# Five kinds of transfers change their issuing engine: from SyncE to GpSimd, in a fused kernel of four layers

## The chip, the core and the metric

The kernel runs on one core of a Trainium2 chip. A core has five engines with an instruction stream of their own: TensorE (PE in the profile, with its weight loads as PEld), VectorE (DVE), ScalarE (ACT), GpSimd (POOL) and SyncE (SP). Sixteen DMA engines move data between the device's memory and the core's on-chip memory. An engine's instructions start in the order of its stream, and a transfer is started by an instruction in the stream of the engine that issues it. The metric is the device time of one execution in microseconds; the profile also gives the clock that TensorE was granted.

## The reference

The input x has shape (16, 32, 128, 128): 16 images of 32 channels. Four layers follow, each of the form x = x + layer(gn(x)), where gn normalises the channels of an image in 16 groups:

```python
x = x + _L0_conv_ref(_gn(x), ...)   # row LSTM over skewed columns: 128 steps of gates
x = x + _L1_conv_ref(_gn(x), ...)   # adder network: -sum |patch - w| over 3x3x32, quantised to 8 bit
x = x + _L2_conv_ref(_gn(x), ...)   # Hartley transform, 32x32 modes mixed across channels, and back
x = x + _L3_conv_ref(_gn(x), ...)   # five edge operators, normalised; small U-shaped net; times its input
```

Layer 3 ends with `return orig * y`, where y comes from conv1 on 160 edge channels, three poolings, conv2 to conv4, and three 2x2 upsamplings each followed by a 3x3 convolution. All outputs are float32.

## The kernel before

The program has three stages in time. `stage0` computes layer 0 for all images. Then `Differences` computes layer 1, image by image, while `After` computes layers 2 and 3 for groups of four images (g = 0 to 3) in the background. What is left when layer 1 ends is done by `drain`.

**Layer 1.** For each half of an image there are 72 tiles (8 groups of output channels by 9 taps) of 128 partitions by 64 rows. A tile is made either by VectorE (L705, a float16 subtract and max into `d_dve`) or by ScalarE (L702, a ReLU into `d_act`), and TensorE sums it over the channels with 16 matmuls (L592). Loads of the quantised image `q` (L559), of raw rows `xq` (L536) and of the residual `xr1` (L566), the store of quantised rows (L552) and the store of the layer's output x2 (L579) are issued by SyncE.

**The background.** `Weave` is a planner at build time. It keeps an estimate in microseconds of where PE, DVE and ACT stand, and places pieces of `After`'s work between the tiles of layer 1. A piece can be put off: `weave.later(us, step)` says that `step` becomes due so many estimated microseconds from now. Transfers are put off this way too, so their place in the stream of the issuing engine follows the plan, and on the chip the issuing engine waits at that place until the transfer may start. Once this is written out, `keep_order` fixes every engine's order as it stands. In the drain, two such planners (one with the rest of groups 0 to 2, one with group 3) take turns, and after that the framework keeps the order of the program.

**A group's way through layers 2 and 3.** `forward` loads x2, transforms it and mixes the modes (loads of mode weights L1114, stores and loads of small matrices L1041, L1092, L1151). It clears its tile `xs` by two GpSimd memsets (L983, L984). `back` transforms the mixed modes back, adds them to x2, 16 pieces of 512 KB a group, and stores x3: `residual` loads a piece (L1169), `take_out` adds and takes statistics on VectorE (L1213, L1215), and `store` writes it back (L1219) and later reloads the buffer for the piece four further on. `encoder` then reads x3 twice. `frames` keeps a ring of two chunks of 20 rows, each 128 partitions by 20 by 132 float32; a half chunk is loaded by `load` (L1277, up to 10 rows of 512 bytes for each partition) and normalised in place by ScalarE (L1283), with edges set by ScalarE copies and, at the first and last row of an image, a GpSimd memset (L1286). The first pass, `statistics`, feeds matmuls at L1323 and copies the image's sides (L1353); the second, `conv1`, feeds matmuls at L1638. After the last half chunks of the first pass the loads of the second pass's first chunks follow. Between them, SyncE loads `gm` (L1311, L1389), which VectorE uses at L1383, and folded weights `v` (L1435), used at L1450. `small_layers` loads its weights at L766 and L835. `last` works on four units of 32 rows: `load` reads x3 in four transfers of 32 partitions each (L1708), TensorE makes the last upsampling (L849, L874), VectorE multiplies (L1766, L1729), ScalarE adds the mean (L1739), and `store` writes the output in four transfers (L1745).

All of these transfers are issued by SyncE, in one stream; only three small constant loads at the start come from ScalarE's queue. GpSimd does memsets and one reduction over partitions.

Of the kernel before, what the change touches and what calls it, by code (L numbers as in the profile page):

```python
# [15 lines left out]
B, C, H, W = 16, 32, 128, 128  # L16
# [27 lines left out]
def bc_view(t, g):  # L44

    return t.rearrange("b c h w -> (b c) (h w)")[g * 128 : (g + 1) * 128]
# [856 lines left out]
class After:  # L903
# [250 lines left out]
    def back(self, g, load):  # L1154


        nc, tc, cst, d, weave = self.nc, self.tc, self.cst, self.d, self.weave
        x2, x3, z_d = d["x2"], d["x3"], d["z"]

        with self.pool("t_z") as zp_, self.pool("t_r", 4) as rp:  # L1160

            def rows(n):

                first = g * 4 * CHW + (4 * (n // 2) + 64 * (n % 2)) * W
                return lambda t: bass.AP(t.tensor, t.offset + first, [[HW, 128], [32 * W, 2], [1, 4 * W]])

            def residual(n):
                xr.append(rp.tile([128, 2, 4 * W], F32, name="xr2"))
                nc.sync.dma_start(xr[n], rows(n)(x2))  # L1169

            xr = []
            stat = zp_.tile([128, 32, 6], F32, name="stat3")
            zi = zp_.tile([128, 32, 32], F32, name="zi")
            for blk in range(4):
                first = z_d.offset + (4 * g + blk) * 32768
                nc.sync.dma_start(
                    zi[32 * blk : 32 * blk + 32], bass.AP(z_d.tensor, first, [[32, 32], [1024, 32], [1, 32]])
                )
            for n in range(4):
                residual(n)  # L1180
            yield -12.0

            o1 = zp_.tile([128, 32, 4, 32], F32, name="o1")
            for oh in range(2):
                pa = [self.acc() for _ in range(4)]
                for o in range(16):
                    for r in range(4):
                        for blk in range(4):
                            part = slice(32 * blk, 32 * blk + 32)
                            nc.tensor.matmul(  # L1190
                                pa[blk][32 * r : 32 * r + 32, 32 * o : 32 * o + 32],
                                zi[part, 16 * oh + o, :],
                                cst["cas_t"][part, 32 * r : 32 * r + 32],
                                start=True,
                                stop=True,
                            )
                    yield 1.1
                yield SUMMED
                for blk in range(4):
                    dst = o1[:, :, blk, 16 * oh : 16 * oh + 16].rearrange("p h o -> p o h")  # L1200
                    src = pa[blk].rearrange("p (o h) -> p o h", h=32)
                    nc.vector.tensor_copy(dst, src)
                weave.dve += 2.6
                yield -2.0

            ready = {}

            def take_out(n, pf):
                while ready.get(n):
                    weave.done(ready[n])  # L1210
                for r in range(2):
                    v = xr[n][:, r]
                    nc.vector.scalar_tensor_tensor(v, pf[r], 2.0**-15, v, ALU.mult, ALU.add)  # L1213
                for r in range(2):
                    nc.vector.bn_stats(stat[:, 2 * n + r, :], xr[n][:, r])  # L1215
                weave.dve += 2.8

                def store():
                    nc.sync.dma_start(rows(n)(x3), xr[n])  # L1219
                    ready[n + 4] = weave.later(6.0, lambda: reload(n + 4)) if n < 12 else None  # L1220

                ready[n + 4] = weave.later(4.0, store)

            def reload(n):
                residual(n)
                ready[n] = None

            previous = None
            for n in range(16):
                s, half = n // 2, n % 2  # L1230
                pf = [self.acc() for _ in range(2)]
                for i in range(4):
                    for r in range(2):
                        part = slice(64 * half + 32 * r, 64 * half + 32 * r + 32)
                        nc.tensor.matmul(  # L1235
                            pf[r][:, W * i : W * i + W],
                            o1[part, 4 * s + i].rearrange("p b o -> p (b o)"),
                            cst["cas_t"][part, :],
                            start=True,
                            stop=True,  # L1240
                        )
                yield 0.8
                if previous:
                    yield -4.5
                    take_out(*previous)
                previous = n, pf
            yield SUMMED
            take_out(*previous)
            weave.later(7.0, lambda: [load(ch, half) for ch in range(2) for half in range(2)])
            mv = zp_.tile([128, 1, 2], F32, name="mv3")  # L1250
            nc.vector.bn_aggr(mv[:, 0, :], stat.rearrange("p a b -> p (a b)"))
            yield from normalised(nc, zp_, self.ps, weave, mv, 1, cst["avg2_bc"], 1e-5, self.stats3)
            nc.vector.scalar_tensor_tensor(
                self.shift3, self.stats3[:, 0], -1.0, self.stats3[:, 1], ALU.mult, ALU.mult
            )
            yield -2.5

    def frames(self, g, pool):

        nc, x3, weave = self.nc, self.d["x3"], self.weave
        ring = [pool.tile([128, 20, W + 4], F32, name=f"xp{i}") for i in range(2)]
        for t in ring:
            nc.vector.memset(t[:, :, 0], 0.0)
            nc.vector.memset(t[:, :, W + 3], 0.0)

        def parts(ch, half):

            lo, hi = max(16 * ch - 2 + 10 * half, 0), min(16 * ch + 8 + 10 * half, H)
            off = lo - (16 * ch - 2)
            return ring[ch % 2], lo, hi, ring[ch % 2][:, off : off + hi - lo, 2 : W + 2]

        def load(ch, half):
            t, lo, hi, v = parts(ch, half)
            nc.sync.dma_start(v, bc_view(x3, g).rearrange("p (h w) -> p h w", w=W)[:, lo:hi, :])  # L1277

        def normalise(ch, half, us):
            t, lo, hi, v = parts(ch, half)  # L1280

            def step():
                nc.scalar.activation(v, v, AF.Identity, bias=self.shift3, scale=self.stats3[:, 1])  # L1283
                for edge, r, src, zero in ((lo == 0, 1, 3, 0), (hi == H, 18, 16, 19)):
                    if edge:
                        nc.gpsimd.memset(t[:, zero, :], 0.0)  # L1286
                        nc.scalar.copy(t[:, r, 2 : W + 2], t[:, src, 2 : W + 2])
                own = slice(10 * half, 10 * half + 10)
                nc.scalar.copy(t[:, own, 1], t[:, own, 3])  # L1289
                nc.scalar.copy(t[:, own, W + 2], t[:, own, W])  # L1290
                weave.act += 2.0

            return weave.later(us, step)

        chunk = lambda ch: ring[ch % 2]
        return load, normalise, chunk

    def statistics(self, g, pool, frames, sides, out, tables):
# [395 lines left out]
    def last(self, g):  # L1694

        nc, tc, cst, weave = self.nc, self.tc, self.cst, self.weave
        with self.pool("l_y") as yp, self.pool("l_x", 2) as xp:
# [3 lines left out]
            def at(t, unit, j):  # L1701
                first = t.offset + g * 4 * CHW + (32 * unit + 8 * j) * W
                return bass.AP(t.tensor, first, [[HW, 32], [CHW, 4], [1, 8 * W]])

            def load(unit):
                xr = xp.tile([128, 4, 8 * W], F32, name="xr3")
                for j in range(4):
                    nc.sync.dma_start(xr[32 * j : 32 * j + 32], at(self.d["x3"], unit, j))  # L1708
                return xr

            xr = [load(0), load(1)]

            rhs = yp.tile([128, 2, 4], F32, name="l_rhs")
            nc.vector.tensor_tensor(rhs, bcast(self.stats3[:, :, 0], 2, 4), bcast(cst["m4_bc"], 1, 2), ALU.mult)
            yield -2.0
            p = self.acc()
# [25 lines left out]

            def store(x, unit):
                for j in range(4):
                    nc.sync.dma_start(at(self.out, unit, j), x[32 * j : 32 * j + 32])  # L1745
                following[unit] = weave.later(10.0, lambda: reload(unit)) if unit < 2 else None

            def reload(unit):
                xr[unit] = load(unit + 2)
                following[unit] = None  # L1750
# [5 lines left out]
            for unit in range(4):  # L1756
                complete(unit - 2)
                x = xr[unit % 2]
# [186 lines left out]
```

## Time and profile before

| What | Value |
|---|---|
| Time, median of 3 runs | 7221.99 us (7218.79 to 7231.17) |
| Span of the profiled execution | 7207.9 us, 272193 instructions |
| Mean granted TensorE clock | 0.891 |
| Busy: PE, PEld | 5763.4 us (80%), 3183.3 us (44%) |
| Busy: DVE, ACT, POOL | 5804.1 us (81%), 5477.6 us (76%), 34.7 us |
| Bytes moved by DMA | 722.55 MB, mean 100 GB/s |
| Transfers at the five lines of the change | 64 each at L1169, L1219, L1708, L1745; 128 at L1277 |

Busy time is what an engine spends on instructions; an instruction that waits, branches or issues a transfer from SyncE or ScalarE is not counted. In groups of instructions, `xr<-acc` names the tile written and the tile read, `x64` is the number of instructions, and after the bar stand the busy time in us, the mean ns of one, the idle time of the engine just before them, and what ended most of it. In the list of waits, a row gives who waited, for whom, the total in us, how many times and the longest. `SPq` means SyncE's queue: all of SyncE's time is waiting or issuing.

### The profile page before, as it was taken

To read this page: it belongs to the slowest core of one execution; us is meant where nothing else is said; L and a number is where in the kernel's file an instruction comes from. 1 tells how busy PE (TensorE), PEld (TensorE's weight loads), DVE (VectorE), ACT (ScalarE), POOL (GpSimd) and SP (SyncE) were. 2 spreads that over 40 slices of the span, in tenths; PEclk is the share of its full clock that TensorE was granted. 3 is DMA by queue.
4 is the path that set the end of the run, shared out by engine and by line. 5 is a ranking of instruction groups with operands and counts; after the bars stand their busy time and mean duration, and the time that the engine had idled before them with its cause. 6 is when DMAs were issued, how large, how long until landed. Compare 5 with 4: busy or idle time off the path is not lost. (4 is left out here: it accounts for less than half of the span.)

```text
span 7207.9 us, 272193 instructions
## 1 busy us (share of the span) xinstructions
PE 5763.4 (80%) x128140; PEld 3183.3 (44%) x128140; DVE 5804.1 (81%) x7016; ACT 5477.6 (76%) x3147; POOL 34.7 (0%) x31
## 2 busy tenths in 40 slices
PE   4878567777888786999778786899888787698985
PEld 3665333333344342333334443333334466546653
DVE  7787689999999998999899998999989882513234
ACT  2555489999999998999999998999999851032322
POOL 0000000000000000000000000000000000000000
PEclk9899889999988898999888988999988876699997
DMA  8664211111133343111253344211134245531234
GB/s 310 227 207 142 84 63 57 56 58 46 48 94 102 127 110 93 64 55 49 53 133 94 99 139 109 72 55 59 35 101 116 85 130 163 163 105 57 65 70 114
DMA packets 374322, 722.55 MB, mean 100 GB/s; under 512 B 50896, under 2 KB 219856, under 8 KB 362320
## 3 DMA queue, kind: packets, MB, share of 16 engines
q1 hardware_dynamic: 372768, 704.58, 31.8%
q8 instruction: 1002, 16.42, 1.0%
q14 instruction: 120, 0.98, 0.0%
q10 hardware_dynamic: 432, 0.57, 0.0%
HBM read 507.21 MB, written 164.32 MB: 93 GB/s over the span
## 5 line engine op out<-in xcount | busy, mean ns | idle before, releaser
L702 ACT ACTIVATE d_act<-q,neg 128x8192 f16<-128x8192 f16 (+1 forms) x622 | 4398.3, 7143 | 204.1 <-PE acc L592 154.9
L705 DVE TENSOR_SCALAR d_dve<-q,qw 128x8192 f16<-128x8192 f16 (+1 forms) x1682 | 3877.4, 2362 | 166.4 <-PE acc L592 124.1
L592 PE MATMUL acc<-d_dve,sel 128*32 128x512 f16 x26912 | 1882.1, 403 | 512.9 <-DVE d_dve L705 458.9
L592 PEld LDWEIGHTS <-sel 128*32 128x32 f16 x36864 | 1027.2, 100 | 2137.7 <-issue 1482.8
L1638 PE MATMUL acc<-xp,wf 32*32 32x512 f32 x25600 | 1034.2, 616 | 36.5 <-issue 26.7
L592 PE MATMUL acc<-d_act,sel 128*32 128x512 f16 x9952 | 732.2, 417 | 315.1 <-ACT d_act L702 306.5
L1638 PEld LDWEIGHTS acc<-xp,wf 32*32 32x32 f32 x25600 | 418.5, 104 | 397.0 <-issue 319.5
L1577 ACT ACTIVATE y<-pooled,b 32x128 f32<-32x128 f32 x512 | 204.7, 400 | 396.3 <-DVE pooled L1563 247.3
L622 PE MATMUL acc<-q,zero 128*32 128x512 f16 x7008 | 503.0, 398 | 0.0
L207 PE MATMUL pg<-h,wb 64*64 64x20 f32 (+15 forms) x4096 | 398.4, 322 | 104.7 <-DVE h L256 63.3
L1283 ACT ACTIVATE xp<-xp,shift,stats 128x1280 f32<-128x1280 f32 (+1 forms) x128 | 182.4, 1434 | 358.2 <-DMA xp<-x_d 356.1
L849 PE MATMUL acc<-y,u_conv 32*32 32x256 f32 (+1 forms) x9728 | 359.4, 466 | 69.7 <-issue 45.1
L244 ACT ACTIVATE gt<-pg,bias 128x20 f32<-128x20 f32 (+15 forms) x1024 | 316.9, 375 | 81.4 <-PE pg L207 74.2
L207 PE MATMUL pg<-e,wb 64*64 64x20 f32 (+15 forms) x4096 | 354.7, 316 | 16.7 <-DVE e L260 5.6
L207 PEld LDWEIGHTS pg<-h,wb 64*64 64x64 f32 x4096 | 250.6, 155 | 139.3 <-DVE h L256 88.7
L622 PEld LDWEIGHTS <-zero 128*32 128x32 f16 x7008 | 211.9, 101 | 195.6 <-issue 40.5
L207 PE MATMUL pg<-xn,wb 64*64 64x28 f32 (+61 forms) x4096 | 286.6, 304 | 11.3 <-ACT gt L244 3.5
L207 PEld LDWEIGHTS pg<-e,wb 64*64 64x64 f32 x4096 | 253.0, 157 | 92.5 <-DVE e L260 62.9
L1323 PE MATMUL acc<-xp 32*64 32x204 f32 (+3 forms) x8576 | 249.9, 359 | 31.3 <-ACT xp L1289 22.9
L255 ACT ACTIVATE th<-c 128x20 f32<-128x20 f32 (+15 forms) x256 | 81.3, 320 | 235.1 <-DVE c L253 233.7
L849 PEld LDWEIGHTS acc<-y,u_conv 32*32 32x32 f32 x9728 | 171.1, 111 | 193.1 <-issue 139.3
L1739 ACT ACTIVATE xr<-xr,l_ms 128x1024 f32<-128x1024 f32 x64 | 70.0, 1141 | 221.9 <-DVE xr L1729 199.3
(208 smaller groups left out, 4607.3 us busy)
## 6 DMA issues: line engine op xcount, KB each, us to landing
xr<-x_d SPq DMA_DIRECT2D x192, 512.0 KB
xp<-x_d SPq DMA_DIRECT2D x112, 640.0 KB
q<-q_d SPq DMA_DIRECT2D x32, 2145.0 KB
x_d<-xr SPq DMA_DIRECT2D x128, 512.0 KB
x_in<-in_x_dram SPq DMA_DIRECT2D x16, 2048.0 KB
res<-in_x_dram SPq DMA_DIRECT2D x64, 512.0 KB
xn<-in_xs_dram SPq DMA_DIRECT2D x64, 512.0 KB
xn<-xn SPq DMA_DIRECT2D x128, 256.0 KB
```

The costliest lines, as they stand in the source:

```text
L207: nc.tensor.matmul(bank[c][q][64 * pair : 64 * pair + 64, :, :width], wb[half, 4 * kind + KIND[q]].rearrange("p b o -> p (b o)"), v[half], ...
L244: nc.scalar.activation(gt[:, q, :, :n], bank[c][q][:, :, :n], AF.Tanh if q == G else AF.Sigmoid, bias=bias[:, KIND[q] : KIND[q] + 1],)
L255: nc.scalar.activation(th[:, :, :n], cell, AF.Tanh)
L592: self.nc.tensor.matmul(acc[k][32 * j : 32 * j + 32, :], self.sel16[:, i // 9, :], d[:, row : row + 4, c : c + W], start=first, stop=last,)
L622: self.nc.tensor.matmul(acc[k][32 * j : 32 * j + 32, :], self.zero, q[:, :4, :W], start=False, stop=False)
L702: nc.scalar.activation(dst, src, AF.Relu, bias=self.neg[:, i : i + 1])
L705: nc.vector.tensor_scalar(dst, src, self.qw[:, i : i + 1], 0.0, ALU.subtract, ALU.max)
L849: nc.tensor.matmul(acc[blk][32 * j : 32 * j + 32, o : o + rows * n], t[part, 4 * par + tap, :], src[part, top : top + rows, left : left + ...
L1283: nc.scalar.activation(v, v, AF.Identity, bias=self.shift3, scale=self.stats3[:, 1])
L1323: nc.tensor.matmul(gram[blk][j : j + width, at : at + n], xp[part, l, 2 + j : 2 + j + width], xp[part, rows, j : j + width + 4], start=sta ...
L1577: nc.scalar.activation(d, s, AF.Identity, bias=bj)
L1638: nc.tensor.matmul(acc[blk][32 * j : 32 * j + 32, :], tap_of("all", tap)[rows], xp[rows, 4 * j + kh : 4 * j + kh + 4, kw : kw + W], start= ...
```

## The change

Five transfer lines are issued by GpSimd instead of SyncE: loads and stores of `back`, loads of `frames`, and loads and stores of `last`. All other transfers stay with SyncE. It is meant to split one stream into two, so that a transfer that has to wait for its engines does not stand before transfers of another part of the program. Sizes, addresses, buffers and the plan are the same.

```diff
             def residual(n):
                 xr.append(rp.tile([128, 2, 4 * W], F32, name="xr2"))
-                nc.sync.dma_start(xr[n], rows(n)(x2))
+                nc.gpsimd.dma_start(xr[n], rows(n)(x2))
...
                 def store():
-                    nc.sync.dma_start(rows(n)(x3), xr[n])
+                    nc.gpsimd.dma_start(rows(n)(x3), xr[n])
...
         def load(ch, half):
             t, lo, hi, v = parts(ch, half)
-            nc.sync.dma_start(v, bc_view(x3, g).rearrange("p (h w) -> p h w", w=W)[:, lo:hi, :])
+            nc.gpsimd.dma_start(v, bc_view(x3, g).rearrange("p (h w) -> p h w", w=W)[:, lo:hi, :])
...
                 for j in range(4):
-                    nc.sync.dma_start(xr[32 * j : 32 * j + 32], at(self.d["x3"], unit, j))
+                    nc.gpsimd.dma_start(xr[32 * j : 32 * j + 32], at(self.d["x3"], unit, j))
...
                 for j in range(4):
-                    nc.sync.dma_start(at(self.out, unit, j), x[32 * j : 32 * j + 32])
+                    nc.gpsimd.dma_start(at(self.out, unit, j), x[32 * j : 32 * j + 32])
```

## The prediction, before the change was run

> **What bounds the kernel now.** I read the slices first, then busy time by stage, then the costliest groups, then who waits for whom, and last single stretches of the trace.
>
> The kernel's page, busy tenths in 40 slices of 180 us, one row an engine:
>
> ```profile
> PE   4878567777888786999778786899888787698985
> ...
> DVE  7787689999999998999899998999989882513234
> ACT  2555489999999998999999998999999851032322
> ```
>
> Three stages: the recurrence (to about 1050 us), the differences of layer 1 with the back work of layers 2 and 3 woven in (to 5860), and a drain (the last 1348 us). The second stage is two thirds of the time, and there VectorE (DVE) and ScalarE (ACT) are both full; in the drain they are a quarter to a half busy and TensorE (PE) leads. Busy us of each engine in the last two stages:
>
> ```profile
> 1050.00:5860.00 4810.00, 3972.41 (x82426) 1902.86 (x82422) 4540.25 (x3610) 4616.92 (x1213) 27.22 (x15) 0.91 0.27 80
> 5860.00:7208.00 1348.00, 1077.25 (x31330) 755.64 (x31322) 460.54 (x1110) 298.12 (x561) 5.10 (x9) 0.81 0.41 113
> ```
>
> After the length come PE, its weight loads, DVE, ACT and POOL (GpSimd): DVE is idle for 4810 - 4540 = 270 us of the second stage, ACT for 193. What fills DVE there, by shape, with the mean ns of one:
>
> ```profile
> L705 DVE TENSOR_SCALAR d_dve<-q,qw 128x8192 f16<-128x8192 f16 x1053 | 2447.4, 2352 | 90.6 <-PE acc L592 89.6
> L705 DVE TENSOR_SCALAR d_dve<-q,qw 128x8320 f16<-128x8320 f16 x576 | 1371.1, 2380 | 35.6 <-PE acc L592 34.5
> ```
>
> 8192 elements a partition in 2352 ns are 3.5 per ns. A float32 subtract of 2048 elements (L1014) takes 2284 ns, 0.9 per ns: L705 runs in a fast mode, some four times as fast an element.
>
> The change is about the queue. SyncE's longest waits in the second stage (us in total, times, longest):
>
> ```profile
> SPq L552 <- DVE qt L549: 939.7, 47, 43.5
> SPq L579 <- DVE xr L573: 697.7, 51, 86.4
> SPq L1277 <- PE acc L1638: 307.8, 11, 65.4
> SPq L1745 <- ACT xr L1739: 199.5, 8, 84.2
> SPq L1219 <- DVE xr L1213: 160.1, 26, 53.2
> ```
>
> It stands for hundreds of us with everything later behind it, and the last three rows move. But what it delays has slack: in this stage ACT waits only 2.8 us in 4 waits for frames (L1283), and DVE's waits for any transfer add up to about 70 us: gm (L1383) 33.0, xw (L1099) 26.1, folded weights (L1450) 8.1, xh 4.0. The queue could return little there.
>
> The last view decides. Two clears by GpSimd, beside DVE:
>
> ```profile
> 3742.00 1.90 POOL L983 MEMSET xs<- 64x2048 f32 x1 [520.21 <-PE acc L849]
> 3743.94 1.99 POOL L984 MEMSET xs<- 64x2048 f32 x1
> ...
> 3742.20 1.99 DVE L549 TENSOR_SCALAR qt<-qt 128x1040 f16<-128x1040 f16 x1
> 3744.11 6.26 DVE L705 TENSOR_SCALAR d_dve<-q,qw 128x8192 f16<-128x8192 f16 x2
> ```
>
> The f16 clamp L549, 0.43 us elsewhere, takes 1.99 and ends with the first clear; the two L705 take 6.26 instead of 4.70. The only three L705 over 2.5 us in the run are about 3.97 us, and all lie at such clears (1566.8, 1570.7 and 3744.1 us). It works both ways: the row clear L1286 takes 0.21 us in the drain and 2.17 to 3.22 in four places beside L705. So DVE's fast mode and GpSimd exclude each other, and here one waits for the other.
>
> [...]
>
> **The change part by part.** 320 transfers move, 80 for each of four groups of images: L1169 16, L1219 16, L1277 32, L1708 16 and L1745 16. By the trace 196 of them are issued before 5860 us (36, 32, 64, 32, 32), 124 in the drain. Bytes and arithmetic stay.
>
> 1. *Lost by DVE in the second stage.* [...] DVE waits h whenever its next instruction is a fast one. The fast ones are busy (3754 + 39 + 26)/4810 = 79% of the stage. h is not shown. Low end: 0.2 us, the shortest row clear, so 196 x 0.2 x 0.79 = 31 us. High end: the frame loads are 1280 pieces of 512 B (128 partitions x 10 rows) where the others have 128 or 256; [...] DVE's 270 idle us hide some 6% of that, leaving 145. Rows behind it cannot overtake: each engine's order in this stage is fixed, PE waits for L705 (287 waits between 1150 and 5890 us) and ACT's next tiles for PE.
>
> 2. *Gained in the second stage.* At 4422 us a 2145 KB q load stands behind frame loads, and then blocks the next issue by 30 us:
>
> ```profile
> 4422.48 0.37 SPq L1277 DMA_DIRECT2D xp<-x_d  x1
> 4423.19 0.55 SPq L559 DMA_DIRECT2D q<-q_d  x1
> 4427.72 0.36 SPq L1277 DMA_DIRECT2D xp<-x_d  x1
> 4428.14 31.14 SPq L1435 DMA_DIRECT2D v<-fold_d  x3
> 4459.38 1.38 SPq L1389 DMA_DIRECT2D gm<-in_gram_dram  x2
> ```
>
> DVE then sits idle for gm for 21.9 us. Without L1277 ahead of it the q load leaves earlier and the jam is likely over. I count 20 us. A like jam at 5582, which costs DVE 22.1 us at L1099, has no moved transfer in it and stays.
>
> 3. *Gained in the drain.* The chain shows two places:
>
> ```profile
> 5995.05 18.12 DMA xm_d<-xm
> 6013.18 0.50 SPq L1092
> ...
> 6015.38 14.83 DMA xp<-x_d
> ```
>
> Frame loads wait behind L1092, which waits for another group's store; PE is idle 22.0 us here, 15 of which go. At 7025.64 to 7030.79 four output stores (L1745) hold up a weight load (L766) for which PE then idles 10.7 us; 10 go. Together 25.
>
> 4. *Lost in the drain.* A frame load takes 4.2 us from issue to ACT's start where nothing else holds it, but the ring is two chunks deep, about three half chunks of 9 us ahead, so 1 to 5 us more stay hidden behind PE's other products. The store-and-reload of back (L1219, L1169) is exposed where PE waits for L1213: [...] the memsets L1286 behind transfers on GpSimd, [...] I take 10 in all.
>
> Frames in the second stage have 14 to 36 us from issue to use in nearly all cases; [...] SyncE's 0.36 us an issue saves nothing: it is idle anyway.
>
> Sum: 145 - 20 - 25 + 10 = +110; with 7222 that is 7332, say 7335.
>
> **The rivals.**
> - *The queue is relieved and DVE loses nothing* [...]: -20 - 25 + 10 = -35, 7187. For it: [...] the waits on SyncE are long. Against: the clears, and that little waits for those transfers.
> - *It cancels*: h at the low end, 31 - 35, 7218.
> - *GpSimd starves instead*: DVE's fast instructions run back to back, [...] With ten turns of 2.35 us a frame lands 24 us late; over a lead of 14 to 20 us that is some 8 us on ACT for each of the 32 loads of statistics in the stage, 250 us, about 7470. For it: L1286 at 3.22 us, 15 times its free time. Against: it still ran after one instruction, not ten.
>
> **How the numbers follow.** DVE loses about a microsecond for each transfer: 0.57, 7335. Relief alone: 0.26, 7187. Cancels: 0.09. Starved: 0.08. Faster by over 0.2% (below 7208) is the second, 0.26; within 0.2%, 0.10; slower 0.64. The range runs from a little below full relief, 7165, as the jams may be worth more than I found, to the high end of h: 357 x 0.94 = 336, less 35, is 7523, [...] part of the starved case, 7550.
>
> **What would show it.** Right: in the second stage the mean L705 rises from 2.36 us, with many at 3 to 4 us; the stage grows by about 110 to 140 us and the drain shrinks by some 15; the gaps at gm and before L766 are gone. POOL shows 320 more instructions of about 1 us. Wrong: L705 keeps its 2.35 us with stage and drain both a little shorter (relief), or keeps it while ACT's idle before L1283 grows in the second stage (starved). It would also be wrong if frames become late in the drain, where I have counted 10 us.

## The result, and the profile after

The changed kernel takes 7276.0 us (median, 7268.1 to 7291.1), beside 7220.4 us for the kernel before in the same comparison: a ratio of 1.0079, 95% interval 1.0057 to 1.0102. It is about 56 us slower, half of the 113 us forecast.

The stretches of the changed kernel's trace, cut where layer 1 ends (5906 us here, 5862 before); after the length come the busy us of PE, its weight loads, VectorE (DVE), ScalarE (ACT) and GpSimd (POOL), then the granted clock, the share of the DMA engines and GB/s:

```profile
1050.00:5906.00 4856.00, 3962.57 (x82557) 1892.41 (x82546) 4558.21 (x3608) 4618.86 (x1213) 354.52 (x211) 0.92 0.27 80
5906.00:7289.00 1383.00, 1071.76 (x31202) 749.18 (x31188) 458.42 (x1109) 294.57 (x561) 143.44 (x197) 0.81 0.39 110
```

The second stage grew by 44 us between these two executions, the drain by 38. That is more than the 56 us of the medians, since the profiled execution of the kernel before (7210.6 us) is a fast one of its kernel and that of the changed one (7291.1 us) the slowest of four. DVE's busy time in the stage rose only from 4542 to 4558 us. GpSimd's issues now count as busy: 355 us in the stage. The groups of L705 and of the moved loads and stores in that stage (busy us, mean ns of one, idle before):

```profile
L705 DVE TENSOR_SCALAR d_dve<-q,qw 128x8192 f16<-128x8192 f16 x1053 | 2458.1, 2362 | 100.3 <-PE acc L592 99.3
...
L705 DVE TENSOR_SCALAR d_dve<-q,qw 128x8320 f16<-128x8320 f16 x576 | 1374.6, 2386 | 51.5 <-PE acc L592 50.0
L1277 POOL DMA_DIRECT2D xp<-x_d x64 | 120.1, 1878 | 1310.4 <-PE acc L1638 917.2 <-PE acc L1323 156.0 <-DVE d_dve L705 69.1
```

L705 went from 2352 to 2362 ns and from 2380 to 2386. A frame load takes GpSimd 1878 ns on average in the stage; in the drain, where no L705 runs, the same instruction takes 0.95 us. One such meeting in the timeline of the changed kernel (start, us, engine and line; "x3" joins three instructions that follow each other):

```profile
2608.32 7.32 DVE L705 TENSOR_SCALAR d_dve<-q,qw 128x8320 f16<-128x8320 f16 x3
2608.94 2.31 POOL L1277 DMA_DIRECT2D xp<-x_d  x1 [7.31 <-PE acc L592]
```

The load starts inside the first L705 and ends 0.6 us after the second began (at 2610.61). The second takes 2.73 us, the others 2.37. So GpSimd waits for the running L705 to end, and then holds the next for 0.4 us. Of the 1682 L705 in this trace, 32 are over 2.5 us beside a frame load, at 2.65 to 2.81 us; over 2.35 us that is 12.3 us in all. No transfer of the other four lines stretches one that far. Seven shorter VectorE instructions beside frame loads of the stage (copies at L1353, clamps at L549) are longer too, by some 3 us together. The clears at L983 and L984 still do, as before; one pair of them now falls beside L705 where it did not, for 3.6 us more.

The jam at the q load is the same, though it looks different. VectorE waits for gm in the changed kernel's timeline:

```profile
4446.59 0.76 SPq L559 DMA_DIRECT2D q<-q_d  x1
4447.40 7.84 SPq L1435 DMA_DIRECT2D v<-fold_d  x3
4471.98 5.35 SPq L1389 DMA_DIRECT2D gm<-in_gram_dram  x2
...
4507.72 0.60 DVE L1383 TENSOR_TENSOR es_w<-acc,gm 128x420 f32<-128x420 f32 x1 [22.98 <-DMA gm<-in_gram_dram]
```

The q load leaves 0.6 us after the last L573 of its image has ended; before, it left 15.6 us after it, with a frame load just ahead. SyncE stands 7.84 us at L1435 instead of 31.14. The queue is relieved, and gm still comes late: DVE waits 22.98 us (21.86 before). Over the whole stage it waits 44.0 us for gm, where it waited 33.0.

In the drain, PE's waits in the kernel before (who, for whom, us in total, times, longest):

```profile
PE acc L1323 <- ACT xp L1289: 22.9, 2, 22.0
...
PE acc L1235 <- DVE xr L1213: 20.6, 10, 6.7
```

and in the changed one:

```profile
PE acc L1235 <- DVE xr L1213: 38.9, 12, 13.4
...
PE acc L731 <- DVE ns_mean L728: 22.3, 2, 21.0
```

The 22 us at the frames behind L1092 are gone, as forecast. In their place PE waits 21 us at L731 for the statistics of group 2's x3, which come late. VectorE's timeline shows a reason that has nothing to do with GpSimd's speed. Before:

```profile
5891.90 6.69 DVE L1014 TENSOR_TENSOR xh<-xh,mr 128x2048 f32<-128x2048 f32 x3
5901.20 1.29 DVE L1213 SCALAR_TENSOR_TENSOR xr<-acc,xr 128x512 f32<-128x512 f32 x2 [2.61 <-DMA xr<-x_d]
```

and after:

```profile
5942.48 0.69 DVE L1213 SCALAR_TENSOR_TENSOR xr<-acc,xr 128x512 f32<-128x512 f32 x1 [10.85 <-DMA xr<-x_d]
...
5948.41 6.67 DVE L1014 TENSOR_TENSOR xh<-xh,mr 128x2048 f32<-128x2048 f32 x3
```

Before, a step of group 3's `forward` (L1014) comes first, while the reload of group 2's fifth piece is under way. After, the take-out of that piece (L1213) comes first, and VectorE waits 10.85 us for the reload with group 3's step behind it. So VectorE's order is not the same in the two kernels. The order is fixed in the stage of layer 1 alone; in the drain the built program does not keep that of the kernel's text, other than the description above says, and about 90 of VectorE's 7016 instructions stand in another place after the change. All six profiles with both loads and stores of back on GpSimd in the drain have the second order, with waits of 10.5 to 11.6 us at this place; the other eight have the first, with 2.6 to 4.7 us.

The drain by milestones, us of each part (L1213 is counted at its start, and the last two columns belong to experiments told below):

| Part of the drain | before | after | frames alone | stores of back on SyncE |
|---|---|---|---|---|
| last L705 to last L1213 of group 2 | 129.1 | 152.9 | 126.9 | 140.1 |
| to first L1213 of group 3 | 193.4 | 177.8 | 197.2 | 183.7 |
| to its last L1213 | 116.4 | 123.9 | 117.5 | 119.7 |
| to the last L1323 (statistics) | 182.3 | 192.1 | 188.6 | 186.7 |
| to the last L1638 (conv1) | 506.9 | 513.7 | 514.7 | 513.5 |
| to the end | 217.6 | 223.0 | 216.1 | 222.5 |
| sum | 1345.7 | 1383.4 | 1361.0 | 1366.2 |

The first row follows that order: it is 151 to 155 us in the six profiles with the second, and 127 to 129 in those with the first, apart from the 140 of the last column. Part of it is made good in the second row. Not every row is a sure difference: in four profiles of kernels with an unchanged drain, named below, the part of conv1 lies between 506.9 and 513.4 us.

### The profile page after: what moved, and what is told of

It is laid out like the page before. It is cut to its first block, busy times and chain, and to the rows that moved or that the text cites. A ratio compares the mean times of both kernels' runs of the same rounds, so it can differ in the third digit from the quotient of the medians.

```text
span 7289.3 us, 272328 instructions
## 1 busy us (share of the span) xinstructions
PE 5746.0 (79%) x128140; PEld 3165.9 (43%) x128140; DVE 5820.4 (80%) x7016; ACT 5476.1 (75%) x3147; POOL 500.4 (7%) x415
## 5 line engine op out<-in xcount | busy, mean ns | idle before, releaser
L705 DVE TENSOR_SCALAR d_dve<-q,qw 128x8192 f16<-128x8192 f16 (+1 forms) x1682 | 3893.3, 2370 | 192.7 <-PE acc L592 149.4
L1638 PE MATMUL acc<-xp,wf 32*32 32x512 f32 x25600 | 1045.0, 619 | 51.9 <-issue 40.5
L1638 PEld LDWEIGHTS acc<-xp,wf 32*32 32x32 f32 x25600 | 419.7, 104 | 416.3 <-issue 339.2
L1283 ACT ACTIVATE xp<-xp,shift,stats 128x1280 f32<-128x1280 f32 (+1 forms) x128 | 182.3, 1434 | 392.3 <-DMA xp<-x_d 189.0
L1277 POOL DMA_DIRECT2D xp<-x_d x128 | 180.5, 1412 | 1923.6 <-PE acc L1638 1270.3
L207 PE MATMUL pg<-xn,wb 64*64 64x28 f32 (+61 forms) x4096 | 286.1, 303 | 10.7 <-ACT gt L244 3.5
L1323 PE MATMUL acc<-xp 32*64 32x204 f32 (+3 forms) x8576 | 243.5, 349 | 20.2 <-issue 20.1
```

The source lines that it names most:

```text
L207: nc.tensor.matmul(bank[c][q][64 * pair : 64 * pair + 64, :, :width], wb[half, 4 * kind + KIND[q]].rearrange("p b o -> p (b o)"), v[half], ...
L705: nc.vector.tensor_scalar(dst, src, self.qw[:, i : i + 1], 0.0, ALU.subtract, ALU.max)
L1277: nc.gpsimd.dma_start(v, bc_view(x3, g).rearrange("p (h w) -> p h w", w=W)[:, lo:hi, :])
L1323: nc.tensor.matmul(gram[blk][j : j + width, at : at + n], xp[part, l, 2 + j : 2 + j + width], xp[part, rows, j : j + width + 4], start=sta ...
L1638: nc.tensor.matmul(acc[blk][32 * j : 32 * j + 32, :], tap_of("all", tap)[rows], xp[rows, 4 * j + kh : 4 * j + kh + 4, kw : kw + W], start= ...
```

## The experiments

One execution of the kernel before can differ from the next by 20 us, and more (36 runs of it lie between 7196 and 7237 us). So for a part of the stage the medians decide. The length of the drain is steadier: 1345.7, 1350.6, 1351.1 and 1352.3 us in the four profiled kernels that left it as it was, 1350 on average.

**Stage alone and drain alone.** All five lines issue on GpSimd only while layer 1 runs, or only in the drain (one line of the first is shown; the second has the two engines the other way round):

```diff
-                nc.sync.dma_start(xr[n], rows(n)(x2))
+                (nc.sync if weave.draining else nc.gpsimd).dma_start(xr[n], rows(n)(x2))
```

> The five kinds of transfers are issued by GpSimd only while layer 1 runs, and by SyncE in the drain. In the profiles of before and after, the last tile of layer 1 lies 42 us later after the change and the rest of the time is added in the drain. Theory 'late transfers' (what moved lands later, and collides on the DMA engines with the loads of layer 1): the stage keeps its share, about +30 to +40 us over before. Theory 'held VectorE' (fast VectorE instructions wait [...]): only the 12 us by which L705 grew beside frame loads, so +10 to +15 us. A third, that the whole difference arises in the drain: 0.

> The reverse: GpSimd issues them only in the drain, 124 of 320. VectorE runs no fast tiles there. Theory 'late transfers': +15 to +30 us over before, from the store-and-reload loop of back. Theory 'held VectorE': 0, or faster by up to 25 us, since a split queue was to return 25 us there. If the two stages add up, this run and the one with the stage of layer 1 alone sum to the change, about +56.

Stage alone: 7238.7 us against 7213.2 before, ratio 1.0033 (1.0023 to 1.0043), +24 us. Drain alone: 7249.0 us, 1.0049 (1.0035 to 1.0063), +35 us; its drain is 1386 us long. So the larger share is lost in the drain, where a gain was forecast, and the stage loses a fifth of the 125 us forecast for it (145 less 20). By its median the drain lost more than either theory expected; the stage's +24 lies between the two, so that run does not decide for one of them. The two add to 59 us, about what the whole change costs: 56 us in the first comparison, and 69 us when the changed kernel was run once more beside them:

> The change itself, beside the other three on the same chip: +45 to +65 us over before, L705 up by 12 us in all, all of it beside frame loads.

It took 7282.0 us, 1.0092 (1.0071 to 1.0113), with a drain of 1383 us and 39 L705 over 2.5 us, both as in the first profile; its time is a little above the range expected.

**What one GpSimd transfer holds.** The kernel before, with four useless transfers from GpSimd behind each frame load of the stage; each of them has as many pieces as a frame load, of 32 bytes (the tile `spare` is made elsewhere):

```diff
             nc.sync.dma_start(v, bc_view(x3, g).rearrange("p (h w) -> p h w", w=W)[:, lo:hi, :])
+            if not weave.draining:
+                for _ in range(4):
+                    nc.gpsimd.dma_start(
+                        spare[:, :, :8], self.a["gram"][:, 0, :80].rearrange("p (r w) -> p r w", w=8)
+                    )
```

> The kernel before, with four extra GpSimd transfers beside each of the 64 frame loads of the layer 1 stage: 128 x 10 pieces of 32 bytes into a tile that nobody reads, 256 in all, [...]. Nobody waits for them. Theory 'held VectorE': each holds the next fast instruction by 0.38 us, as a frame load does, so up to 256 x 0.38 x 0.79 = 77 us more. Theory 'late transfers': within 15 us of before, as no transfer that anyone waits for has moved. If GpSimd only waits and never holds, L705 stays at 2.36 us.

7325.1 us, 1.0156 (1.0138 to 1.0174), +112 us, more than either theory expected. Beside the 256 added transfers 123 L705 are over 2.5 us long; over 2.35 us that is 46.9 us in all, or 0.38 us each, one L705 for about every second transfer, as beside the 64 frame loads. So VectorE is held, and in proportion, by a transfer of 1280 pieces for 0.38 us. Another large part of the loss is in another place, ScalarE's waits in the stage of this kernel (L1292 is L1286 here, L1295 the copy after it):

```profile
ACT xp L1295 <- POOL xp L1292: 107.9, 2, 68.1
```

The small clear of an edge row stands in GpSimd's stream behind transfers that wait (here for each other, 1039.9 us in 252 waits, since all write the one tile `spare`), and ScalarE with its 7 us tiles of layer 1 waits for the clear: 108 us in two places. The two sums may overlap, so they do not divide the 112 us. The wait is a cost of one engine's order, which no busy time shows.

**Each part by itself.** Only the frame loads on GpSimd; only loads and stores of back; only loads and stores of last:

```diff
# frames alone: L1277; back alone: L1169 and L1219; last alone: L1708 and L1745
-            nc.sync.dma_start(
+            nc.gpsimd.dma_start(
```

> Only the loads of frames (L1277) go to GpSimd, 128 of the 320 transfers. These hold VectorE for the 12 us that L705 grew, so at least +10 us if that is not hidden. In the drain a frame load lands in 4.5 us instead of 4.2, ahead of need. Theory 'late transfers' with back as the place: +10 to +20 us here, the rest with back. If frames are the place: +40 or more.

> Only the loads and stores of back (L1169, L1219) go to GpSimd, 128 transfers. After the change the take-out of pieces in the drain started at the moment their reload landed, in a ring of four; before, it had 3 us a piece. Theory 'late transfers' with back as the place: +25 to +40 us, most of it after the last tile of layer 1. Theory 'held VectorE': 0, as these hold nothing (L705 grew beside frame loads alone).

> Only the loads and stores of last (L1708, L1745) go to GpSimd, 128 transfers of 32 partitions each. Theory 'late transfers' with back as the place: within 10 us of before. If the stores no longer standing before the weights of small_layers (L766) are worth what was forecast, 10 us less than before. If the loads colliding with the rows of layer 1 (ScalarE waited 7 us for xq at 3681 us) matter: +10 to +20.

Against 7214.2 us: frames 7232.5, ratio 1.0022 (1.0013 to 1.0031), +16 us; back 7221.0, 1.0011 (1.0003 to 1.0019), +8; last 7221.4, 1.0010 (1.0002 to 1.0018), +7. Drains of 1361.0, 1358.7 and 1349.1 us. Only the first shows L705 stretched by transfers, 12 us in all as in the whole change; and its drain is 9 to 15 us longer than an unchanged one, so that of its +16 us only 1 to 7 would be left for the stage. The split is rough: the drain is that of one execution, 7211.6 us, the fastest of the 22. If it holds, a good part of the hold lies in time that VectorE would have waited anyway; no run shows this by itself. Back, where 25 to 40 us had been expected, costs 8. The three sum to 31 us, 25 to 38 less than the whole. Against the 1350 us of an unchanged drain the three add 11, 9 and -1 us, and the whole change 33: part of what is missing comes in the drain, when they are moved together, and part in the stage.

**All but the frames.** To see which part brings the surplus:

```diff
-            nc.gpsimd.dma_start(v, bc_view(x3, g).rearrange("p (h w) -> p h w", w=W)[:, lo:hi, :])
+            nc.sync.dma_start(v, bc_view(x3, g).rearrange("p (h w) -> p h w", w=W)[:, lo:hi, :])
```

> The change, but with the frame loads (L1277) left on SyncE. Alone the parts cost +16 (frames), +8 (back) and +7 us (last), 31 in all, and the whole change +56 to +69. Theory A (the rest comes from frames sharing GpSimd's stream with back and last, where one waits behind another): without the frames the others cost their own sum, +15 us or less, about 7229 us, so that the frames make 41 to 54 us of the whole. Theory B (back and last hinder each other as much): +30 us or more, 7245 us. Theory C (it is the frames' own 16 us and no sharing): +40 to +53 us.

7235.7 us against 7216.6, 1.0033 (1.0019 to 1.0048): +19 us by medians, +24 by the ratio. The sum of back and last is 15 us; the interval, 14 to 35 us, reaches from theory A to theory B, so how far these two hinder each other stays open. In the drain they seem to: it is 1367.0 us long, 17 more than an unchanged one, where alone they add 9 and -1. The frames, added to them, cost 32 to 50 us, where alone they cost 16. What differs most in the stage is ScalarE's wait for raw rows (xq, L536, issued by SyncE), before and after:

```profile
ACT xq L540 <- DMA xq<-x_d: 12.2, 4, 4.9
...
ACT xq L540 <- DMA xq<-x_d: 37.7, 4, 15.1
```

It is 4.6 us with the frames alone, 8.1 without the frames, but 23.5 (stage alone), 28.7 and 37.7 us in the three profiles with all five lines on GpSimd there. It is no full account: with only the stores of back left on SyncE (told below) it is 10.5 us, and there ScalarE waits 17.0 us for the clear of an edge row (L1286), a wait of which the first profile of the changed kernel has none and the second 5.4 us.

**The q load in four.** One instruction reads 32 channels four times over into 128 partitions. Here it is written as four transfers, in the kernel before and in the changed one:

```diff
-        self.nc.sync.dma_start(q, bass.AP(q_d.tensor, first, [[0, 4], [(H + 2) * P, C], [1, (self.R + 2) * P]]))
+        for k in range(4):
+            self.nc.sync.dma_start(
+                q[32 * k : 32 * k + 32], bass.AP(q_d.tensor, first, [[(H + 2) * P, C], [1, (self.R + 2) * P]])
+            )
```

> The kernel before, with the q load (2145 KB, four copies of 32 channels by a step of zero) as four transfers of 32 partitions. After the change gm was issued 35 us before it landed though SyncE was free, so the jam at 4480 us lies in the DMA engines' queues behind the q load and not in the order of issue. [...] the jam goes: VectorE's waits for gm and xw (33 and 26 us before) fall below 15 together, and the time by 30 to 60 us. If the jam is one of bytes, nothing changes.

> The change, with each q load (L559) written as four transfers of 32 partitions. Theory A (part of what the change costs are collisions of GpSimd's transfers with the long q load, and those are now shorter): the distance to the kernel before with q in four (7157.6 us) falls to the +35 us that the drain alone cost, so 7190 to 7197 us. Theory B (the cost has nothing to do with the q load): the distance stays at the change's +56 to +69 us, so 7213 to 7227 us. Either way the wait of VectorE for gm behind the q load (22.98 us in the changed kernel) should fall below 5 us, since in the kernel before with q in four it did.

With all else as before: 7157.6 us against 7214.2, 0.9921 (0.9905 to 0.9937), 57 us faster, and the fastest kernel of this study. First the jam. The stretch of the changed kernel in which gm has been issued and has not come:

```profile
4477.00:4507.00 30.00, 3.64 (x32) 1.27 (x32) 7.50 (x10) 18.63 (x3) 0.00 (x0) 0.51 0.26 75
```

and the first 10 us after the same q load in the kernel before with q in four:

```profile
4390.00:4400.00 10.00, 6.23 (x194) 3.17 (x182) 8.51 (x9) 10.00 (x3) 0.00 (x0) 1.00 1.02 230
```

The last two numbers of each line are the share of the 16 DMA engines and the rate in GB/s (a packet counts where it starts, so a short stretch can pass 1). A mean share of 0.26 moves 75 GB/s for 30 us while gm stands behind; with the load in four parts the share is 1.02, at 230 GB/s. DVE no longer waits for gm, and its wait for xw falls from 26.1 to 5.4 us. So the jam was in the DMA engines, behind the q load, and the change of the issuing engine did not end it.

Not all of the 57 us is the jam, though. Layer 1's very first q load is faster too, ahead of the stage that the prediction looked at. VectorE's first L705 in the kernel before, and the same instruction (L708 there) with q in four:

```profile
921.25 16.03 DVE L705 TENSOR_SCALAR d_dve<-q,qw 128x8192 f16<-128x8192 f16 x7 [40.20 <-DMA q<-q_d]
...
895.79 41.02 DVE L708 TENSOR_SCALAR d_dve<-q,qw 128x8192 f16<-128x8192 f16 x18 [17.45 <-DMA q<-q_d]
```

VectorE waits 23 us less here, and layer 1 ends 62 us earlier in this profile. So a good part of the gain is a shorter start of layer 1, outside the jam.

The changed kernel with q in four takes 7203.5 us against 7216.6, 0.9983 (0.9977 to 0.9990). To its counterpart that is +46 us, between theory A's 35 and theory B's 56 to 69. VectorE has no wait for gm left, as both expected. ScalarE's waits for xq in the stage of this kernel:

```profile
ACT xq L540 <- DMA xq<-x_d: 6.6, 2, 5.8
```

37.7 us in the changed kernel, 6.6 here (12.1 in the counterpart): these waits are gone, and the distance is 10 to 23 us smaller than the change's 56 and 69. Its size fits a collision of GpSimd's transfers with the long q load, but the intervals of the two ratios are 5 and 12 us wide on each side, so I call it likely, not shown. The loss in the drain stays: 1394.0 us in this profile, 42 more than the counterpart's 1352.3.

**Stores of back on SyncE.** The change, with one line taken back:

```diff
-                    nc.gpsimd.dma_start(rows(n)(x3), xr[n])
+                    nc.sync.dma_start(rows(n)(x3), xr[n])
```

> The change, but with the store of back (L1219) left on SyncE. Theory A (in the drain a store of back stands on GpSimd's stream behind a reload that waits for an earlier store to land, and so comes late): the end of back for group 2 after layer 1's last tile returns from 153.6 us to 130 to 140 us, PE's waits at L1235 for L1213 shrink from 38.9 to about 25 us, and the time falls 10 to 15 us below the change's. Theory B (only the later landing of each GpSimd transfer counts): a store on SyncE lands some 0.5 us earlier and nothing else moves: within 5 us of the change, group 2's end stays near 150 us.

GpSimd's stream in the changed kernel's drain shows the case:

```profile
5943.56 0.73 POOL L1169 DMA_DIRECT2D xr<-x_d  x1 [3.56 <-DMA x_d<-xr]
5944.28 0.72 POOL L1219 DMA_DIRECT2D x_d<-xr  x1
5946.38 0.73 POOL L1169 DMA_DIRECT2D xr<-x_d  x1 [1.37 <-DMA x_d<-xr]
5947.10 0.72 POOL L1219 DMA_DIRECT2D x_d<-xr  x1
```

A reload (L1169) waits until the store of its buffer has landed, and a later store (L1219) is issued the moment the reload is out. But these two stores are late by only 0.45 and 0.35 us, counted from the end of the take-out that they wait for. Over the 32 stores of the drain this lateness is 0.30 us in the median and 60 us in sum; in the kernel before it is 1.44 and 115, and in this one, with the stores on SyncE, 1.16 and 144. So GpSimd's stores do not come late, and what theory A says of the cause is refuted. With the stores in another stream PE's waits in the drain become

```profile
PE acc L1235 <- DVE xr L1213: 23.5, 9, 13.7
...
PE acc L731 <- DVE ns_mean L728: 17.9, 2, 16.8
```

The first falls from 38.9 us to 23.5, back of group 2 ends at 140.1 instead of 152.9 us, and the drain is 17 us shorter, as the table shows. Theory A's numbers came out, for another reason than its own: with this line taken back VectorE's order at the fifth piece is the first one again, and it waits 4.58 us there. How much of the 17 us the order makes is open: back alone has the second order too, and a drain only 9 us longer than an unchanged one. The change with VectorE's old order was not run. A rest stays, for the drain is still 16 us longer than an unchanged one. The time, 7262.6 us against 7216.6, 1.0072 (1.0057 to 1.0087), +46 us, is 10 below the change's first measurement and 23 below its second. Its own runs spread from 7241 to 7288 us, so the time alone would not have decided it.

**Later frames without GpSimd.** The kernel before, all on SyncE, with a small load into the same place ahead of each frame load of the drain, which has to wait for it:

```diff
+            src = bc_view(x3, g).rearrange("p (h w) -> p h w", w=W)[:, lo:hi, :]
+            if weave.draining:
+                nc.sync.dma_start(v[:, :1, :8], src[:, :1, :8])
-            nc.sync.dma_start(v, bc_view(x3, g).rearrange("p (h w) -> p h w", w=W)[:, lo:hi, :])
+            nc.sync.dma_start(v, src)
```

> The kernel before, all on SyncE, but in the drain each frame load (L1277) has a small transfer of 8 elements a partition into the same place ahead of it, for which it must wait: each lands some 2 to 3 us later, and GpSimd issues nothing. Theory A (the frames' cost in the drain is the later landing, about 0.9 us a load for +13 us): two to three times that, +25 to +40 us in the drain, the time near 7245 to 7260 us. Theory B (the drain hides later frames, and the +13 us came from GpSimd's stream itself, its waits and memsets): within 10 us of the kernel before.

SyncE's waits in this kernel's drain (L1280 is the frame load):

```profile
SPq L1280 <- DMA xp<-x_d: 96.9, 26, 7.7
```

26 loads were held back by 3.7 us on average; the rest found the small load landed. The time is 7215.8 us against 7216.6, 1.0002 (0.9994 to 1.0011), and the drain 1355.6 us. From GpSimd a frame comes 0.9 us later (0.6 for the issue, 0.3 from there to ScalarE). A delay four times as long, at 26 of 64 loads, cost 3 to 10 us of drain and nothing in the medians. So 0.9 us of later landing can hardly make the frames' 9 to 15 us of drain: theory B by its number. That GpSimd's stream makes them is not shown by this. In the kernel with the frames alone 21 of VectorE's and 11 of ScalarE's instructions stand in another place than before, here 15 and 28, so the order is a rival that these runs leave untested.

## Why the prediction was half right

The sign was right, and the loss that the forecast was built on exists; the sum was wrong: +110 was 145 - 20 - 25 + 10, and the runs give about +24 for the stage and +35 for the drain. That the sum came out no further off is in part luck: 125 us were forecast for the stage, five times too many, and the drain, forecast to gain 15 us, lost more than the stage.

1. *Lost by DVE in the second stage, 145 us: the term of the sum that failed.* That the frame loads hold VectorE's fast instructions stands, as the spare transfers show (0.38 us each). But h, the hold by one transfer, was an estimate that no trace had shown: counted at 196 x 0.79 places, it is 0.38 us at 32, all beside the 64 frame loads and none beside the 132 others: 12 us in all (15 with shorter instructions), below the low end of 31. GpSimd's instruction takes 0.95 us for a frame load alone, and an L705 is held for less than half of that, once for every two loads. With it falls the high end, 357 us, which was not shown either: the frame loads' 1280 pieces cost 0.95 us to issue. The hold goes both ways: 0.95 us becomes a median of 2.04 for GpSimd in the stage, 2.35 becomes 2.73 for VectorE.
2. *Gained in the stage, -20 us: did not come.* The q load did leave earlier, as the step said. But the jam is in the DMA engines, at a share of 0.26 for the 30 us behind this load, and gm came 23 us late again. The step read a wait at SyncE (31.14 us at L1435) as the cause, where it was a second victim. Instead ScalarE waits 11 to 25 us longer for xq in the three profiles with all five lines, which the forecast didn't have.
3. *Gained in the drain, -25 us: half right.* The 22 us at L1323 went, and came back as 21 us at L731 and 18 more at L1235, in a drain whose VectorE runs in another order. The other place did not gain, as the chain of the changed kernel shows:

```profile
7091.86 11.81 PE acc L1486 x270
...
7103.79 12.38 DMA w_conv<-in_conv_dram
7116.17 0.14 issue
7116.31 7.62 PE acc L1486 x262
```

No store stands ahead of the weight load (L766) now. It still starts only when the convolution that reads its buffer ends, and takes 12.4 us to land instead of 8.1 (why is open): PE waits 12.7 us, 10.7 before. Of those 10.7 us the stores of the kernel before made 2.5, from the end of the convolution at 7028.4 us to the load's start at 7030.9; the rest was the load's own time to land.
4. *Lost in the drain, +10 us: mis-sized.* With step 3's gain paid back it is about +35 net, +38 in the profile. What the step took for each trip of back through memory was an estimate that no trace had shown. It left out that the build orders the drain anew when lines move: with loads and stores of back on GpSimd VectorE waits 10.85 us for one reload ahead of group 3's work, 2.61 before. Taking the stores back restores that order and returns 17 us of the 38. The stores themselves are earlier than before, so it is not the trips through memory. Frames it took to be almost wholly hidden; alone on GpSimd they cost 9 to 15 us of drain.
5. *The rivals.* Relief alone is refuted: each of the kernels in which only lines of the change moved is slower. Cancelling is too, though its low end for h was nearer than what the sum took. Starving is refuted: with its waits a frame load takes GpSimd 2.04 us in the median, which leaves room for one L705, not ten, and ScalarE waits 0.6 us for frames in the stage (2.8 before).

What stays open: whether the 12 us of hold in the stage cost so little with the frames alone, how the 24 us of the stage divide between the hold, xq and the clears, what the new order alone costs in the drain, and whether the frames' part of it comes from GpSimd's waits or from the order.

## What to carry to other kernels

A long wait at an issuing engine is a cost only if what stands behind it is needed: follow it to the instruction that ends last, and ask whether the engines that carry the transfer are free. Where a load is slow, look at the share of DMA engines while it runs (0.26 here) before its place in a queue; rewriting one load gave 57 us, where moving 320 transfers lost 56. Before transfers move to an engine's stream, look whether a small instruction there, such as a clear, has an expensive reader. And where the order of instructions is not fixed, compare the order of every engine before and after: here VectorE's changed though no line of its own did, and the experiments on the drain compare two things at once.

## What the runs showed of the hardware

- GpSimd needs 0.54 us to issue a transfer of 128 pieces (L1708, L1745), 0.73 for 256 (L1169, L1219) and 0.95 for 1280 (L1277), in the drain, where no L705 runs; that is far from ten times for ten times the pieces. SyncE took 0.37 us for L1277.
- Beside VectorE's fast instructions a frame load takes GpSimd 2.04 us (median of 64), and 32 L705 beside such loads are 0.38 us longer. In the changed kernel transfers of 128 and 256 pieces lengthened none past 2.5 us.
- In the drain a frame that nothing else holds up reaches ScalarE 4.5 us after GpSimd has issued it, 4.2 after SyncE.
- The DMA engines moved 75 GB/s at a share of 0.26 behind one q load in one part, and 230 GB/s at a share of 1.02 for four loads of a quarter each.
